# Tail of a fused cross-attention and state-space kernel: dummy products dropped, two comparisons reduced to a largest difference, five row tiles fetched ahead

## The chip, the core and the metric

The kernel runs on one core of a Trainium2 chip, in one launch. The metric is the device time of a whole execution in microseconds (us); where several executions were timed, the median stands for them. A profile of one further execution shows what each engine did: PE (the matrix engine; PEld is its weight load), DVE (vector), ACT (scalar), POOL (GpSimd) and SP, which issues nearly all DMAs.

## What is computed

```python
x = builder_state                       # 4096 x 512; base_state is 3202 x 512, 8 heads of 64
x1 = x + mha(layernorm(x), layernorm(base_state))        # softmax attention, then W_o
U = (layernorm(x1) @ W_in.T + b_in) @ Bmat               # 4096 x 64
def step(s, u_t):                       # one state of 64 numbers, 4096 steps in sequence
    s = silu(s @ A.T) + u_t
    return s, s
states = scan(step, zeros, U)
out = x1 + states @ Cmat + (program_probs.mean(1) @ W_prog.T + b_prog)
```

Everything is float32.

## The kernel before

**Attention.** The 4096 rows are cut into 8 blocks `Q` of 512 and each block into two halves; with 4 pairs of heads this gives 64 *units*, each of 13 *steps* over the keys. A step of a unit is a group of score products (`s`, line 1144), one exponential on ACT (`p`, line 1222), one addition on DVE (`acc`, line 1230) and a group of value products (`po`, line 1280). Keys and values come back from DRAM (`kd`, `vd`) step by step: `load_k` (line 432) is issued with the scores of ten steps earlier (`AHEAD_K`), `load_v` (line 440) six steps ahead of the scores (`AHEAD`), and the value product follows the scores by about four steps (`LAG`). In the last block the units run first over the first halves of the four head pairs and then over the second halves, and every unit loads its own keys and values.

**Rows.** The projected rows `x1`, with the modulation added, are stored in DRAM (`x1d`, lines 1732 and 1843). The inputs `U` of the scan stay in SBUF as `u`.

**The scan.** The 4096 steps are cut into 2 x 128 chunks of L = 16 steps, and all chunks advance together. A first sweep "a" (tile `za`) runs beside the last units from zero states and leaves a guess of each chunk's end in `end1`; a second sweep "b" (tile `z`) starts from those guesses, takes 16 steps `j`, and leaves its ends in `end0`. A step is a product on PE (line 1960), a tanh on ACT (line 1988) and a combination on DVE (line 1995). The last 256 rows, which the attention finishes last, have a short scan of their own (`zl`, `hl`, `sl`; pieces named `l.`).

**The output rows.** Row tile `j` (`rows[j]`, 128 x 2 x 512) holds the rows `16 c + j` of all chunks `c`, for `v` = 0 and 1, the two halves of the sequence; its `v` = 1 part has 112 rows, since the last 256 rows go another way. `fetch(j)` (line 1921) reads it from `x1d` after the last keys and values are loaded. When sweep "b" has finished step `j`, `states` (POOL, line 2027) and `products` (PE, line 2034) make the scan's share, and it is added to the row tile in one of two ways: for two of three `j`, ACT copies the `v` = 1 part (`copied`, line 2048) and POOL adds it (`added`, line 2051), and DVE adds the `v` = 0 part (`joined0`, line 2054); for the third, DVE adds both. SP stores both parts (line 2059). Products of even `j` lie in the PSUM tiles `py_n` and `py_o`, those of odd `j` in the two banks of one tile `pd_last`. The last 256 rows (`xr_l`) are made by two products (`last_ys`, line 2254), added on DVE (line 2257) and stored, the first half by SP and the second by ACT (line 2261).

**The check.** A program-wide number `nbad` says whether the guesses were good enough. `largest` (lines 2073 and 2074) takes the largest absolute value of the new ends and scales it by a tolerance into `top`; `differ` subtracts the old from the new (line 2079, DVE), takes absolute values (line 2081, ACT), compares each with `top` (line 2083, DVE) and counts (line 2084, DVE). This is done for "b" (128 columns) and for "l" (32 columns). `counted` (PE, line 2433) sums the counts over the partitions, `number` (line 2440) subtracts them from what they should be, and all engines load the result (line 2613) and branch past a general version when it is zero.

**What sets the order.** Each operation is a *piece* with an engine, an estimated cost, what it must follow, rings that it takes and a due time, shifted by a table. `Plan.order` simulates the engines with these numbers and writes the pieces out in the order in which the simulation starts them; each engine then executes its own pieces strictly in that order.

**Dummy products.** `idle_` (line 2239) multiplies `a_t` by itself into the scan's PSUM tile; three such pieces (`WARM` = 17 to 19) follow the last steps of the short scan and the end of sweep "b".

Of the kernel before, what the change touches and what calls it, by code (L numbers as in the profile page):

```python
# [13 lines left out]
AF = mybir.ActivationFunctionType  # L14
# [21 lines left out]
WARM = 17  # L36
# [6 lines left out]
NA = 7  # L43
HALF = 18
# [188 lines left out]
def xattn_ssm_kernel(  # L233
# [884 lines left out]
    def alt_tile(k, name):  # L1118
        return alt.tile([P, 2, H], F32, tag=f"alt{k}", name=name)
# [802 lines left out]

    def last_fetch():

        t = x_tile("xr_l")
        for g in range(2):
            r = LAST + g * P
            nc.sync.dma_start(t[:, g], x[r : r + P, :])
            xl.append(t[:, g])

    def open_scan():
# [15 lines left out]
        for name, n in (  # L1947
            ("end0", NCK + 1), ("end1", NCK + 1), ("ul", PRE + 1 + P), ("hw", P), ("hl", P),
            ("sl", P + 1), ("df", NCK), ("st", P // LT),
            ("top", 1), ("bad", 1), ("badl", 1), ("badr", 1),  # L1950
        ):
            sv[name] = two[:, at_ : at_ + n]
            at_ += n
# [122 lines left out]
    def differ(new, old, n, bad):  # L2076

        top, df, ok = sv["top"], sv["df"][:, :n], sv["ok"][:, :n]
        nc.vector.tensor_tensor(df, new, old, ALU.subtract)
        yield  # L2080
        nc.scalar.activation(df, df, AF.Abs)
        yield
        nc.vector.tensor_scalar(ok, df, top, None, ALU.is_le)
        nc.vector.tensor_reduce(bad, ok, AX.X, ALU.add)
# [32 lines left out]
    def last_rows(plan, d):  # L2117
# [121 lines left out]
        def idle_():  # L2239
            for k in range(2):  # L2240
                nc.tensor.matmul(sv["z"][1][:, k, :], a_t, a_t, start=True, stop=True)
# [98 lines left out]
    def drain(plan):  # L2340
# [66 lines left out]
        for name, new, old, count, bad, of in (  # L2407
            ("b", lambda: sv["end0"][:, 1:], lambda: sv["end1"][:, 1:], NCK, "bad", [("b", "end")]),
            ("l", lambda: sv["sl"][:, : P : LT], lambda: sv["st"], P // LT, "badl",
             [("l.near", 0), ("l.near", 1), "l.from", ("differ", "b", 2)]),  # L2410
        ):

            v = {}
# [23 lines left out]
        def number():  # L2437
            sv["nbad"] = small.tile([1, 1], I32, tag="nbad", name="nbad")
            all_ = P * (NCK + P // LT + 3 * len(units))
# [3 lines left out]
        plan.add("counted", "PE", 300, counted, ["risen", ("differ", "l", 2), *free[1]], d)  # L2443
# [169 lines left out]
    n = nc.values_load(sv["nbad"][0:1, 0:1], min_val=0, max_val=P * (NCK + P // LT + 3 * len(units)))  # L2613
# [88 lines left out]
```

## Time and profile before

| | us |
|---|---|
| median of 3 runs (lowest, highest) | 1889.19 (1888.89, 1890.3) |
| the profiled execution | 1889.67 |
| its span, first to last instruction | 1887.9 |
| outside the span | 1.77 |
| PE busy, DVE busy, ACT busy, POOL busy | 1873.1, 1563.3, 1166.6, 258.2 |

The profiled execution is 0.48 us above the median. PE's clock was granted at 0.999 over the span. Times in the text are from the start of the span. A row of the timeline gives start, duration, engine and line, operation, what is written and read, the count of instructions merged into it, and in brackets how long the engine had been idle and what ended that.

### The profile page before, as it was taken

The page shows a single profiled execution, that of the slowest core. Times are in us where ns is not written, and L with a number is a line of the kernel's source. Part 1 is how long each engine was busy: PE and PEld are TensorE (multiplying, and loading weights), DVE is VectorE, ACT ScalarE, POOL GpSimd, SP SyncE. Part 2 cuts the span into 40 slices and gives each one's busy share as a digit, 9 for nine tenths or more (in the row PEclk, how much of TensorE's full clock was granted, in tenths as well). Part 3 has the DMA queues.
Part 4 walks back from the last instruction along what each step waited for, and adds up shares of the span by engine and source line. Part 5 has one row for each costly group of instructions (what it writes and reads, how often), then busy time and mean ns, then how long its engine had stood idle before and what let it go on. Part 6 is the DMA issues. An engine that isn't in the chain of part 4 may idle for free.

```text
span 1887.9 us, 69209 instructions
## 1 busy us (share of the span) xinstructions
PE 1873.1 (99%) x29856; PEld 1414.9 (75%) x29856; DVE 1563.3 (83%) x2142; ACT 1166.6 (62%) x1663; POOL 258.2 (14%) x386
## 2 busy tenths in 40 slices
PE   9999999999999999999999999999999999999997
PEld 5887689777777777797777777777777777777684
DVE  6642699788988889798978898898979897989776
ACT  3242577665766577565756676757757575757653
POOL 6120300022000210022002200021002200110105
PEclk9999999999999999999999999999999999999999
DMA  8554133133323333233313332324313331536477
GB/s 257 158 159 120 54 102 92 38 115 90 106 74 105 86 112 97 65 95 111 98 44 108 87 114 79 106 79 117 98 55 98 107 104 44 171 108 182 139 190 238
DMA packets 260770, 207.58 MB, mean 110 GB/s; under 512 B 94632, under 2 KB 233896, under 8 KB 260460
## 3 DMA queue, kind: packets, MB, share of 16 engines
q1 hardware_dynamic: 256440, 196.48, 36.1%
q10 hardware_dynamic: 4020, 6.62, 1.2%
q8 instruction: 237, 3.88, 0.8%
q14 instruction: 73, 0.60, 0.1%
HBM read 156.32 MB, written 29.88 MB: 99 GB/s over the span
## 4 chain that ended last, share of the span: by engine, by line
PE 97%; DVE 1%; ACT 1%; DMA 0%; issue 0%; POOL 0%; SPq 0%; DVEq 0%; ACTq 0%; POOLq 0%
PE po L1280 37%; PE s L1144 36%; PE pax L404 3%; PE qx L404 3%; PE qy L404 2%; PE pay L404 2%; PE pkx L404 2%; PE pvx L404 2%; PE pvy L404 1%; PE pky L404 1%; PE pk L722 1%; PE pv L599 1%; PE pd L1309 1%; PE sm L1164 1%; PE po L1268 1%; PE pu L1747 1%
## 5 line engine op out<-in xcount | busy, mean ns | idle before, releaser
L1222 ACT ACTIVATE p<-s,shifts 128x1024 f32<-128x1024 f32 (+1 forms) x832 | 891.4, 1081 | 418.3 <-PE s L1144 392.7
L1230 DVE TENSOR_TENSOR acc<-p,acc 128x1024 f32<-128x1024 f32 (+1 forms) x704 | 851.0, 1214 | 96.8 <-ACT p L1222 77.2
L1144 PE MATMUL s<-q,k 64*64 64x256 f32 x12800 | 850.6, 376 | 0.2 <-ACT p L1222 0.2
L1280 PE MATMUL po<-p,v 64*64 64x256 f32 x12800 | 848.2, 376 | 1.0 <-DVE o L1335 0.9
L1144 PEld LDWEIGHTS s<-q,k 64*64 64x64 f32 x12800 | 518.9, 133 | 175.2 <-ACT p L1222 13.5
L1280 PEld LDWEIGHTS po<-p,v 64*64 64x64 f32 x12800 | 519.9, 133 | 163.1 <-issue 3.5
L1634 POOL TENSOR_TENSOR xr<-xr,rowb 128x512 f32<-128x512 f32 x28 | 35.7, 1274 | 797.6 <-DVE acc L1230 688.9
L1358 DVE RECIPROCAL rd<-rd 128x256 f32<-128x256 f32 (+1 forms) x64 | 110.0, 1719 | 6.4 <-ACT rd L1353 6.4
L1249 ACT COPY swap<-acc 64x256 f32<-64x256 f32 x126 | 50.8, 403 | 64.9 <-DVE acc L1237 61.8
L1230 DVE TENSOR_TENSOR acc<-p,p 128x1024 f32<-128x1024 f32 x64 | 78.2, 1222 | 11.6 <-ACT p L1222 11.5
L1729 POOL TENSOR_TENSOR xr<-x,modb 128x512 f32<-128x512 f32 x28 | 41.6, 1496 | 253.3 <-DVE acc L1254 178.3
L1420 POOL TENSOR_SCALAR rstd_x<-mv_x 128x1 f32<-128x1 f32 x28 | 18.6, 666 | 276.7 <-DVE mv_x L1417 276.0
L1215 DVE TENSOR_TENSOR acc<-x,acc 2x256 f32<-2x256 f32 x128 | 54.9, 429 | 1.5
L1254 DVE TENSOR_TENSOR acc<-swap,acc 64x256 f32<-64x256 f32 x126 | 52.4, 416 | 2.9 <-ACT swap L1249 1.3
L1570 ACT ACTIVATE q<-qx,bias 128x256 f32<-128x256 f32 x42 | 17.6, 470 | 48.0 <-PE qx L404 48.0
L582 DVE TENSOR_TENSOR ks<-pky,ks 128x512 f32<-128x512 f32 x15 | 10.4, 692 | 43.2 <-PE pky L404 23.7
L576 ACT ACTIVATE ks<-pkx,bias 128x256 f32<-128x256 f32 x40 | 16.8, 470 | 44.4 <-PE pkx L404 32.9
L1237 DVE TENSOR_TENSOR acc<-acc 128x512 f32<-128x512 f32 x63 | 43.1, 684 | 0.3
L1335 DVE TENSOR_TENSOR o<-po,o 128x256 f32<-128x256 f32 x64 | 27.0, 423 | 14.1 <-ACT o L1331 13.5
L481 DVE STREAM_TRANSPOSE x<-xh_y 128x512 f32<-128x512 f32 x28 | 18.2, 688 | 21.7 <-ACT xh_y L1428 14.7
L1353 ACT ACTIVATE rd<-pd 128x128 f32<-128x128 f32 x126 | 34.0, 275 | 1.0 <-PE pd L1309 0.4
L1178 DVE TENSOR_REDUCE m<-sm 128x1 f32<-128x256 f32 x64 | 24.0, 417 | 11.3 <-PE sm L1164 11.3
(314 smaller groups left out, 1760.7 us busy)
## 6 DMA issues: line engine op xcount, KB each, us to landing
k<-kd SPq DMA_DIRECT2D x432, 128.0 KB, 2.2
v<-vd SPq DMA_DIRECT2D x432, 128.0 KB, 2.2
xn<-x SPq DMA_DIRECT2D x448, 32.0 KB, 1.9
xr<-in_x_dram SPq DMA_DIRECT2D x30, 256.0 KB, 3.2
x1d<-xr SPq DMA_DIRECT2D x30, 256.0 KB, 2.2
x<-in_x_dram SPq DMA_DIRECT2D x28, 256.0 KB, 3.0
cx<-in_ctx_dram SPq DMA_DIRECT2D x25, 256.0 KB, 4.2
kd<-ks SPq DMA_DIRECT2D x20, 256.0 KB, 2.3
```

The lines of the kernel that those rows point to most:

```text
L404: nc.tensor.matmul(to[:, b, :], still[:, i, b * P : (b + 1) * P], moving[:, i, :], start=(start and b == 0 and i == 0), stop=(i == 1), ski ...
L1144: nc.tensor.matmul(s[k0 : k0 + HD, a, b, :], kts[(*w["at"][:2], c)][r, b * CK + k0 : b * CK + k0 + HD], q[r], start=True, stop=True, skip_ ...
L1215: made = nc.vector.tensor_tensor(to[r], t[r], to[r], ALU.add)
L1222: nc.scalar.activation(t[:, :, :nb, :], w["ps"][c][:, :, :nb, :], AF.Exp, bias=w["shift"])
L1230: return nc.vector.tensor_tensor(w["acc"][:, :, :nb, :], t[:, :, :nb, :], before[:, :, :nb, :], ALU.add)
L1237: return nc.vector.tensor_tensor(acc[:, :, 0, :], acc[:, :, 0, :], acc[:, :, 1, :], ALU.add)
L1249: nc.scalar.copy(w["swap"][r], of[(1 - k) * HD : (2 - k) * HD])
L1254: made = nc.vector.tensor_tensor(of[r], w["swap"][r], of[r], ALU.add)
L1280: nc.tensor.matmul(w["po"][k][a * HD : (a + 1) * HD, :QU], vts[Q, hp, c][r, b, a * HD : (a + 1) * HD], t[r, a, b, :], start=(c == 0 and b ...
L1358: nc.vector.reciprocal(w["rd"][:, part], (w["pd"] if last else w["rd"])[:, part])
L1634: return nc.gpsimd.tensor_tensor(xs[half][:, t], xs[half][:, t], rowb, ALU.add)
L1729: return nc.gpsimd.tensor_tensor(xt[:, t], x1[:, t], modb, ALU.add)
```

## The change

The diff has three parts.

1. **No dummy products.** `WARM`, `idle_` and its three pieces go.
2. **Comparisons by the largest difference.** `differ` becomes three DVE instructions in a row: the subtraction, a largest absolute value over the columns into one number a partition (`far`), and one comparison of `far` with `top`, whose result is the partition's count. ACT's absolute value, the comparison of all columns and the sum go, and what was three pieces for each comparison is one. The expected sum changes from `P * (NCK + P // LT + ...)` to `P * (2 + ...)`.
3. **Early rows.** For `j` = 0 to 4 (`NE`), `fetch_early` reads the `v` = 0 part and the first 96 rows of the `v` = 1 part while the last block is computed, as soon as the block before it has been stored and the tile's other users are done. `fetch_late` reads the other 16 rows at the old place.

```diff
-WARM = 17
+NE = 5
...
+    def fetch_early(j):
+
+        rows[j] = alt_tile(j, f"row_{j}")
+        for v, n in enumerate((NCK, END - QU // L)):
+            nc.sync.dma_start(rows[j][:n, v, :], x1r[v, j, :n])
+
+    def fetch_late(j):
+
+        c = slice(END - QU // L, END)
+        nc.sync.dma_start(rows[j][c, 1, :], x1r[1, j, c])
...
     def differ(new, old, n, bad):
 
-        top, df, ok = sv["top"], sv["df"][:, :n], sv["ok"][:, :n]
+        top, df, far = sv["top"], sv["df"][:, :n], sv["far"]
         nc.vector.tensor_tensor(df, new, old, ALU.subtract)
-        yield
-        nc.scalar.activation(df, df, AF.Abs)
-        yield
-        nc.vector.tensor_scalar(ok, df, top, None, ALU.is_le)
-        nc.vector.tensor_reduce(bad, ok, AX.X, ALU.add)
+        nc.vector.tensor_reduce(far, df, AX.X, ALU.max, apply_absolute_value=True)
+        nc.vector.tensor_tensor(bad, far, top, ALU.is_le)
...
-        def idle_():
-            for k in range(2):
-                nc.tensor.matmul(sv["z"][1][:, k, :], a_t, a_t, start=True, stop=True)
-
-        for t in range(WARM, PRE + LT):
-            plan.add(("l.idle", t), "PE", 430, idle_, [("l.z", t), ("b", "h", L - 1)], d)
...
+        before = NQB - 2
+        kept_rows_ = [("row", before, t, "store") for t in range(NT)]
+        used = [("sevenths", NQB - 1, k) for k in CHAIN], [("outs", before, k) for k in CHAIN]
+        for j in range(NE):
+            plan.add(("early", j), "SP", 1000, partial(fetch_early, j), kept_rows_ + used[int(j > 1)] + [from_(d - 36 * STEP)],
+                     d + (2 * j - 36) * STEP)
         for j in range(L):
-            plan.add(("fetch", j), "SP", 100, partial(fetch, j),
-                     ["fetch", ("product", n, j // 2)], d + (5 + j / 2) * STEP, ["p"] if j >= NA else [])
+            plan.add(("fetch", j), "SP", 100, partial(fetch_late if j < NE else fetch, j),
+                     ["fetch", ("product", n, j // 2)] + ([("early", j)] if j < NE else []),
+                     d + (5 + j / 2) * STEP, ["p"] if j >= NA else [])
...
-            def first(new=new, old=old, count=count, bad=bad, v=v):
+            def compare(new=new, old=old, count=count, bad=bad):
                 largest(new())
-                v["d"] = differ(new(), old(), count, sv[bad])
-                next(v["d"])
-
-            costs = (720, 280, 640) if count == NCK else (560, 200, 440)
-            for i in range(3):
-                plan.add(("differ", name, i), "ACT" if i == 1 else "DVE", costs[i],
-                         partial(lambda v, *_: next(v["d"], None), v) if i else first,
-                         [("differ", name, i - 1)] if i else of,
-                         d + (8 * STEP if name == "b" else 0))
+                differ(new(), old(), count, sv[bad])
+
+            plan.add(("differ", name, 0), "DVE", 1300 if count == NCK else 1050, compare, of, d + (8 * STEP if name == "b" else 0))
```

The order moves at three places only. On every engine, all instructions ahead of them stand as before.

The first place is DVE's last rows ahead of the loading of `nbad`. `row_24516` and `row_24519` are row tiles 14 and 15 before, `row_24521` and `row_24524` the same tiles now; `scan` holds all of the check's small tiles. Before:

```order
L2054 SCALAR_TENSOR_TENSOR row_24516<-py_o_24586,row_24516 112x512
L2073 TENSOR_REDUCE scan<-scan 128x1
L2079 TENSOR_TENSOR scan<-scan 128x128
L2054 SCALAR_TENSOR_TENSOR row_24516<-py_n,row_24516 128x512
L2083 TENSOR_SCALAR scan<-scan 128x128
L2054 SCALAR_TENSOR_TENSOR row_24519<-pd_last,row_24519 128x512
L2079 TENSOR_TENSOR scan<-scan 128x32
L2257 SCALAR_TENSOR_TENSOR xr_l<-py_a,xr_l 128x512
L2083 TENSOR_SCALAR scan<-scan 128x32
L2257 SCALAR_TENSOR_TENSOR xr_l<-py_o_24587,xr_l 128x512
L2440 TENSOR_SCALAR nbad<-pd_last 1x1
```

The same place on DVE now:

```order
L2065 SCALAR_TENSOR_TENSOR row_24521<-py_o_24591,row_24521 112x512
L2084 TENSOR_REDUCE scan<-scan 128x1
L2090 TENSOR_TENSOR scan<-scan 128x128
L2091 TENSOR_REDUCE scan<-scan 128x1
L2092 TENSOR_TENSOR scan<-scan 128x1
L2259 SCALAR_TENSOR_TENSOR xr_l<-py_a,xr_l 128x512
L2090 TENSOR_TENSOR scan<-scan 128x32
L2259 SCALAR_TENSOR_TENSOR xr_l<-py_o_24592,xr_l 128x512
L2065 SCALAR_TENSOR_TENSOR row_24521<-py_n,row_24521 128x512
L2065 SCALAR_TENSOR_TENSOR row_24524<-pd_last,row_24524 128x512
L2442 TENSOR_SCALAR nbad<-pd_last 1x1
```

Both additions into the `v` = 0 parts of tiles 14 and 15 moved behind both comparisons and both additions into `xr_l`; of each comparison only one of its several small rows is shown the second time. ACT's copy of tile 15 stood behind DVE's addition of tile 15 and waits for the products alone now, and that addition waits for the copy.

The second place is PE's end, from the last product of tile 14 on (`py_n`, `py_o`). Before:

```order
L2034 MATMUL py_o_24586<-c_21416,scan 64x256
L2241 MATMUL z<-a_t 128x128 x6
L2034 MATMUL pd_last<-c_21416,scan 64x256 x8
L2254 MATMUL py_a<-c_21416,scan 128x512
L2254 MATMUL py_o_24587<-c_21416,scan 128x512
L2433 MATMUL pd_last<-ones,scan 1x1 x3
```

PE's end now:

```order
L2045 MATMUL py_o_24591<-c_21416,scan 64x256
L2256 MATMUL py_a<-c_21416,scan 128x512
L2256 MATMUL py_o_24592<-c_21416,scan 128x512
L2045 MATMUL pd_last<-c_21416,scan 64x256 x8
L2435 MATMUL pd_last<-ones,scan 1x1 x3
```

The dummy products (`z<-a_t`) are gone, and the two products of the last rows moved ahead of the products of tile 15 (`pd_last`).

The third place is SP's queue in the last block, behind the store of a row tile of that block (`xr_23194`); `k_2_1_3` is the key load of head pair 2, second half, step 3. Now:

```order
L1843 DMA x1d<-xr_23194 128x512
L1927 DMA row_23495<-x1d 128x512
L1927 DMA row_23495<-x1d 96x512
L1927 DMA row_23530<-x1d 128x512
L1927 DMA row_23530<-x1d 96x512
L432 DMA k_2_1_3_23533<-kd 128x256
L440 DMA v_1_1_12_23535<-vd 128x128
L1927 DMA row_23559<-x1d 128x512
L1927 DMA row_23559<-x1d 96x512
L432 DMA k_2_1_4_23564<-kd 128x256
```

Before, the load of `k_2_1_3` followed the store directly; tiles 3 and 4 are fetched two and four pairs of loads later, ahead of `k_2_1_6` and `k_2_1_8`. At the old place, five DMAs of 16 rows stand where ten of 128 and 112 rows stood. At the very end of SP's queue, the `v` = 0 stores of tiles 14 and 15 moved behind the store of `xr_l` and the `v` = 1 store of tile 15, and are now the last two.

More of the change, by code (lines that the diff above doesn't have):

```diff
@@ L1949, in open_scan @@
             ("sl", P + 1), ("df", NCK), ("st", P // LT),
-            ("top", 1), ("bad", 1), ("badl", 1), ("badr", 1),
+            ("top", 1), ("far", 1), ("bad", 1), ("badl", 1), ("badr", 1),
         ):
@@ L2409, in drain @@
             ("l", lambda: sv["sl"][:, : P : LT], lambda: sv["st"], P // LT, "badl",
-             [("l.near", 0), ("l.near", 1), "l.from", ("differ", "b", 2)]),
+             [("l.near", 0), ("l.near", 1), "l.from", ("differ", "b", 0)]),
         ):
-            v = {}
-            def first(new=new, old=old, count=count, bad=bad, v=v):
+            def compare(new=new, old=old, count=count, bad=bad):
                 largest(new())
-                v["d"] = differ(new(), old(), count, sv[bad])
-                next(v["d"])
-            costs = (720, 280, 640) if count == NCK else (560, 200, 440)
-            for i in range(3):
-                plan.add(("differ", name, i), "ACT" if i == 1 else "DVE", costs[i],
-                         partial(lambda v, *_: next(v["d"], None), v) if i else first,
-                         [("differ", name, i - 1)] if i else of,
-                         d + (8 * STEP if name == "b" else 0))
+                differ(new(), old(), count, sv[bad])
+            plan.add(("differ", name, 0), "DVE", 1300 if count == NCK else 1050, compare, of, d + (8 * STEP if name == "b" else 0))
         def risen():
@@ L2438, in number @@
             sv["nbad"] = small.tile([1, 1], I32, tag="nbad", name="nbad")
-            all_ = P * (NCK + P // LT + 3 * len(units))
+            all_ = P * (2 + 3 * len(units))
             nc.vector.tensor_scalar(sv["nbad"], sv["py"][1][0][0:1, 0:1], -1.0, float(all_), ALU.mult, ALU.add)
         plan.add("risen", "DVE", 760, risen, [("fall", n), ("rise", n), ("l.kept", 1)], d + STEP)
-        plan.add("counted", "PE", 300, counted, ["risen", ("differ", "l", 2), *free[1]], d)
+        plan.add("counted", "PE", 300, counted, ["risen", ("differ", "l", 0), *free[1]], d)
         plan.add("number", "DVE", 150, number, ["counted"], d)
@@ L2612, in xattn_ssm_kernel @@
                     mybir.DependencyClass.Sync, mybir.DependencyReason.SCHED_ONLY), reason="shared port")
-    n = nc.values_load(sv["nbad"][0:1, 0:1], min_val=0, max_val=P * (NCK + P // LT + 3 * len(units)))
+    n = nc.values_load(sv["nbad"][0:1, 0:1], min_val=0, max_val=P * (2 + 3 * len(units)))
     with tc.If(n > 0, label="general"):
```

## The prediction

> **What bounds the kernel now.** I read the page first: engines, then the chain that ended last.
>
> ```profile
> span 1887.9 us, 69209 instructions
> PE 1873.1 (99%) x29856; PEld 1414.9 (75%) x29856; DVE 1563.3 (83%) x2142; ACT 1166.6 (62%) x1663; POOL 258.2 (14%) x386
> PE 97%; DVE 1%; ACT 1%; DMA 0%; issue 0%; POOL 0%; SPq 0%; DVEq 0%; ACTq 0%; POOLq 0%
> ```
>
> PE is busy for 99% of the span and makes 97% of the chain. No part of the change takes work from PE before 1875 us, and the order of every engine stands as before up to there but for SP. So there are two questions: do the early fetches on SP make PE wait, and what do the last ten microseconds lose or gain. Next I read the end of the timeline.
>
> ```profile
> 1875.96 1.60 PE L2241 MATMUL z<-a_t 128*128 128x128 f32 x12
> 1876.47 1.26 POOL L2051 TENSOR_TENSOR row<-y_l,row 112x512 f32<-112x512 f32 x1
> 1876.53 1.36 DVE L2001 TENSOR_TENSOR scan<-scan,u 128x128 f32<-128x128 f32 x1
> 1877.50 1.09 PE L2034 MATMUL pd_last<-c,scan 64*64 64x256 f32 x16
> 1878.52 0.69 PE L2254 MATMUL py_a<-c,scan 64*128 64x512 f32 x1
> 1878.70 0.28 DVE L2073 TENSOR_REDUCE scan<-scan 128x1 f32<-128x128 f32 x1
> 1879.02 0.15 DVE L2074 TENSOR_SCALAR scan<-scan 128x1 f32<-128x1 f32 x1
> 1879.09 0.28 DVE L2079 TENSOR_TENSOR scan<-scan 128x128 f32<-128x128 f32 x1
> 1880.40 0.68 DVE L2054 SCALAR_TENSOR_TENSOR row<-pd_last,row 128x512 f32<-128x512 f32 x1
> 1881.17 0.60 ACT L2048 ACTIVATE y_l<-pd_last 128x512 f32<-128x512 f32 x1 [1.46 <-DVE row L2054]
> 1881.85 1.26 POOL L2051 TENSOR_TENSOR row<-y_l,row 112x512 f32<-112x512 f32 x1 [4.12 <-ACT y_l L2048]
> 1882.02 1.13 DVE L2083 TENSOR_SCALAR scan<-scan 128x32 f32<-128x32 f32 x1
> 1883.18 0.19 DVE L2084 TENSOR_REDUCE scan<-scan 128x1 f32<-128x32 f32 x1
> 1883.29 0.68 DVE L2257 SCALAR_TENSOR_TENSOR xr_l<-py_o,xr_l 128x512 f32<-128x512 f32 x1
> 1883.88 0.14 DVE L2440 TENSOR_SCALAR nbad<-pd_last 1x1 int32<-1x1 f32 x1
> 1884.00 0.37 ACTq L2261 DMA_DIRECT2D out_dram<-xr_l  x1
> ```
>
> From 1878 us on DVE is the engine that ends last: it goes from one row to the next until 1883.97, and ACT then issues the last store. The rows of line 2261 and of SP's final waits say what follows.
>
> ```profile
> DMA to landing us min/median/max: 2.3/2.3/2.3
> L2614 SPq EVENT_SEMAPHORE  x8: 17/17/17, 1885.6 to 1886.5; - x8
> ```
>
> That store lands at 1884.00 + 2.3 = 1886.3; SP's eight waits for the DMA queues end right after it, at 1886.5, and the closing barrier ends the span at 1887.9. **The end is the landing of the last store plus 1.6 us**, and the last store hangs on DVE's last large addition.
>
> **Part by part.** *Early fetches.* They add ten DMAs to SP between the key and value loads. Each tile brings 128 + 96 rows of 2 KB, so the five bring 2.29 MB. Rows of the stages:
>
> ```profile
> 1765.00:1770.00 5.00, 5.00 (x116) 3.81 (x112) 3.17 (x4) 3.90 (x6) 0.00 (x0) 1.00 0.71 216
> 1770.00:1775.00 5.00, 5.00 (x88) 3.45 (x80) 4.58 (x5) 3.10 (x4) 0.00 (x0) 1.00 0.69 207
> 1775.00:1780.00 5.00, 5.00 (x95) 3.60 (x96) 4.57 (x4) 3.42 (x9) 1.28 (x1) 1.00 0.37 120
> 1825.00:1830.00 5.00, 5.00 (x103) 5.00 (x99) 5.00 (x7) 3.17 (x4) 0.00 (x0) 1.00 1.05 252
> 1766.53 0.38 SPq L432 DMA_DIRECT2D k<-kd  x1
> 1827.30 0.86 PE s L1144 x16
> 1828.16 0.86 PE po L1280 x16
> ```
>
> The last two columns are the share of the DMA engines and GB/s. Full DMA engines move 252 GB/s (1825 us), so 2.29 MB take 2.29 / 0.252 = 9.1 us of them. At 1765 to 1780 us they are not full, so I take 9.1 us as the most by which a load behind all ten fetches is late (the least is 0, if the free share takes them all); ten issues of 0.38 us lie within it. What hides it is the lead of the loads. A step costs PE 0.86 + 0.86 = 1.72 us; keys are issued ten steps ahead, 17 us, and values six steps and the lag of four, also 17 us. 17 − 9.1 leaves 8 us, so I take **0** from a range of 0 to 9.1, and PE stays at 5.00 of 5.00. At the old place, 1816 to 1844 us, SP's row of fetches becomes shorter:
>
> ```profile
> 1816.41 27.85 SPq L1921 DMA_DIRECT2D row<-x1d  x32
> POOL xr_l L2349 <- DMA xr_l<-in_x_dram: 41.7, 1, 41.7
> 1851.94 0.68 DVE L2054 SCALAR_TENSOR_TENSOR row<-py_n,row 128x512 f32<-128x512 f32 x1
> ```
>
> The first tile is added at 1851.94, more than seven microseconds after the last fetch was issued (1816.41 + 27.85 = 1844.3), and the only wait for a DMA among all waits from 1815 us to the end is that of `xr_l`, which is fetched ahead of the rows in both versions. Nobody waits for the rows, so earlier rows gain **0**.
>
> *Dummy products.* Twelve matmuls of 1.60 us go at 1875.96. They stood ahead of tile 15's products, whose inputs were there by about 1876.6: the last of them, DVE's addition of tile 13, stands just ahead of L2001, and the states just ahead of POOL's row at 1876.47. The two products of the last rows take the dummies' place. How long until PE starts what follows them no row shows; the last of them begins to end 0.69 us after the start, and tile 15's 16 matmuls held PE for 1.02 (1877.50 to 1878.52), so it is between these and I take 1.0. They run from 1875.96, tile 15's products then from 1877.0 to 1878.1, **0.5 us earlier** than 1877.50 + 1.09. Does the clock hold without them? It is the number ahead of the last two in each row:
>
> ```profile
> 1881.00:1882.00 1.00, 0.17 (x2) 0.09 (x2) 0.97 (x5) 0.71 (x2) 0.15 (x1) 1.00 0.87 322
> 1883.00:1884.00 1.00, 0.24 (x4) 0.14 (x4) 0.96 (x4) 0.00 (x0) 0.11 (x1) 0.86 0.79 297
> ```
>
> PE's last large products began at 1878.52; the clock is still full at 1881 to 1882 and falls between 1883 and 1884. After the change no gap of a microsecond lies ahead of tile 15's products, so I take 0. [...]
>
> *The copy of tile 15.* ACT's copy no longer stands behind DVE's addition (it started at 1881.17 for that reason). It starts right behind tile 15's products, at about 1878.15, and ends 0.60 later, and POOL's addition starts 0.08 after it (1881.85 against 1881.77 before): 1878.85 to 1880.1. Before, it lay at 1881.85 to 1883.11.
>
> *The shared stall.* While POOL adds two SBUF tiles, some DVE instructions stand still. L2001 took 1.36 us, and L2083 took 1.13, and both ended right after POOL did. An earlier place tells which kinds do:
>
> ```profile
> 1703.54 2.51 POOL L1729 TENSOR_TENSOR xr<-x,modb 128x512 f32<-128x512 f32 x2
> 1704.96 0.38 DVE L1361 TENSOR_REDUCE rises<-rd 128x1 f32<-128x256 f32 x1
> 1705.26 1.07 DVE L1369 TENSOR_TENSOR o<-o,rd 128x256 f32<-128x256 f32 x1
> 1827.77 0.41 DVE L1369 TENSOR_TENSOR o<-o,rd 128x256 f32<-128x256 f32 x1
> ```
>
> A reduction beside POOL takes no longer; a TENSOR_TENSOR from SBUF waits until POOL is done (1.07 against 0.41 us). L2083's stall goes: 1.13 less some 0.2, as 32 columns take (the reduction at 1883.18 took 0.19), is 0.93. But the subtraction of comparison "b" would start at 1879.09 and meets POOL's addition at its new place: it ends about 1880.25 instead of 1879.37. **The stall of 0.93 us goes and one of 0.9 us comes**: 0 together.
>
> *DVE's remaining work.* From 1878.70 on the same additions are left in both versions, so I count the difference. The comparisons of all columns go, 0.28 (as for the subtraction of 128 columns) and 0.2. The sums become largest differences over the same columns, 0. Two comparisons of one column come; no row shows one, the nearest is the 128x1 TENSOR_SCALAR of 0.15, with 0 and the 0.28 of 128 columns as bounds: + 0.3. An instruction that needs the one ahead starts 0.04 after its end (1878.70 + 0.28, then 1879.02), one that doesn't starts 0.08 before it (1879.17, then 1879.09); two more pairs are of the first kind now, 2 × 0.12 = + 0.24. Together − 0.48 + 0.30 + 0.24 = + 0.06, and with the stalls + 0.03: **DVE ends where it ended**, at 1884.0.
>
> *The last store.* It was the second half of `xr_l`, issued alone; the store ahead of it was issued 0.86 us earlier. Now three stores of 256 KB are ready within 1.3 us (`xr_l` at about 1882.7, tile 14 at 1883.4, tile 15 at 1884.0). Rows:
>
> ```profile
> 1883.14 0.33 SPq L2059 DMA_DIRECT2D out_dram<-row  x1
> 1882.00:1883.00 1.00, 0.01 (x1) 0.00 (x0) 1.00 (x2) 0.00 (x0) 1.00 (x1) 1.00 0.83 320
> DMA to landing us min/median/max: 3.1/3.7/5.0
> ```
>
> At 320 GB/s a store of 262 KB costs 0.82 us, three cost 2.5. Behind each other they push the last landing from 2.3 us after its issue to between 2.3 (no queue) and 3.1 (the least of the stores of line 2059 after 1870 us). I take 2.7, between the two, since the queue is short by then: +0.4. Tile 15's store also sits on a queue that SP waits for early, so more of the eight waits follow it: about +0.1.
>
> *The count.* `counted` writes where tile 15's addition reads, so it follows it now: if its six tiny matmuls take half a microsecond, `nbad` ends near 1884.7 instead of 1884.02. From there to SP's first wait at 1885.6 was 1.6 us, so the waits begin near 1886.3, ahead of the landing at 1886.7: covered, 0.
>
> **Sum** against the profiled execution: fetches 0, DVE's end 0, landing 0.4 and waits 0.1, together +0.5, 1889.67 to 1890.2. That execution lay 0.48 above the median of 1889.19, so for the median I say **1889.7 us**.
>
> **Rivals.** (a) *The stall misses.* If ACT's copy comes later and POOL starts behind the subtraction, only the one-column comparison can meet it; DVE ends up to 0.9 us earlier and the stores spread out: −0.5 us, 1888.7. For it: 0.25 us decide. Against it: even then POOL holds until 1880.6 and the comparison of "b" waits.
>
> (b) *The early fetches starve PE* (slower). SP is one queue, and loads stand behind fetches. Once a load is held up so long that it lands after its lead of 17 us, PE loses a microsecond for each further one. For it: the DMA engines are at 0.7 already, and a landing takes some 2.3 us beside the hold-up (as at line 2261). Against it: the bytes are worth 9.1 us. It decides from a hold-up of 17 − 2.3 = 14.7 us on; at two and a half times 9.1, it gives 22.8 + 2.3 − 17 = +8: 1897.
>
> (c) *The dummies were needed.* If PE's clock falls to half without them, the products of the last rows and of tile 15 take twice 1.0 and 1.09: +2.1, 1891.8. For it: PE has pauses all through the tail. Against it: the rows on the granted clock above.
>
> (d) *Faster*: less DMA traffic from 1816 to 1844 lets some access in the tail run quicker. No wait in the profile shows one; the row tiles would have to be late by 4 us, and 1889.2 − 4 = 1885.2 results.
>
> **How the numbers follow.** Forecast 0.60, (a) 0.25, (b) 0.06, (c) 0.05, (d) 0.04. Within 0.2% means within 3.8 us, about what a measurement of this kernel can tell from no change; the forecast, (a) and (c) lie there. Faster 0.04, same 0.89, slower 0.07. The range takes in (a) with the runs' own spread of 0.3 below, the forecast with a full queue at the end (+0.4 more, and 1.1 of spread above): 1888.4 to 1891.2.
>
> **What would show it.** POOL's last addition near 1879 to 1880 and the subtraction beside it at 1.1 us instead of 0.28 (the stall); the last matmuls of tile 15 done near 1878.1; DVE's last large addition ending at 1884.0, with a landing 2.7 us later; PE at 5.00 of 5.00 from 1765 to 1815 us. It is wrong if PE waits for a key or value after 1766 us, if the subtraction takes 0.28 us, or if the clock falls below 1.00 before 1878 us.

## The result, and the profile after

The changed kernel takes **1891.98 us** (median of 21 runs, 1891.17 to 1892.86), the kernel before took 1889.14 us beside it (21 runs, 1888.77 to 1890.76). The ratio is 1.0014, with a 95% interval from 1.0008 to 1.0020: 2.84 us slower, and outside the range of the prediction. The profiled execution took 1892.13 us; these are two lines of its page.

```profile
span 1890.3 us, 69189 instructions
PE 1870.7 (99%) x29844; PEld 1413.6 (75%) x29844; DVE 1562.8 (83%) x2142; ACT 1167.0 (62%) x1661; POOL 258.2 (14%) x386
```

The span grew by 2.4 us while PE does less than before. So the loss isn't work; it must be looked for in the order and the waits of the end. The timeline of the changed kernel's last 15 us (start, duration, engine, line, operation, tiles):

```profile
1875.61 1.35 DVE L2012 TENSOR_TENSOR scan<-scan,u 128x128 f32<-128x128 f32 x1
1876.11 1.09 PE L2045 MATMUL pd_last<-c,scan 64*64 64x256 f32 x16
1877.33 0.60 ACT L2059 ACTIVATE y_l<-pd_last 128x512 f32<-128x512 f32 x1
1878.00 1.26 POOL L2062 TENSOR_TENSOR row<-y_l,row 112x512 f32<-112x512 f32 x1 [1.19 <-ACT y_l L2059]
1878.17 1.24 DVE L2090 TENSOR_TENSOR scan<-scan 128x128 f32<-128x128 f32 x1
1879.77 0.16 DVE L2092 TENSOR_TENSOR scan<-scan 128x1 f32<-128x1 f32 x1
1882.01 0.37 ACTq L2263 DMA_DIRECT2D out_dram<-xr_l  x1
1882.49 0.68 DVE L2065 SCALAR_TENSOR_TENSOR row<-pd_last,row 128x512 f32<-128x512 f32 x1
1883.55 0.15 DVE L2442 TENSOR_SCALAR nbad<-pd_last 1x1 int32<-1x1 f32 x1 [0.38 <-PE pd_last L2435]
```

The order is the one that was set out with the change, and the subtraction beside POOL's addition took 1.24 us. But `nbad` ends at 1883.70, which is 0.32 us earlier than before, and still the span ends 2.4 us later. What lies between are only the load of `nbad` by every engine, the branch on it, and the closing barrier. These are SP's own waits from 1884.5 us on, first of the kernel before, then of the changed one (waiting line, what ended the wait, us in total, times, longest):

```profile
SPq L2614 <- SPq L2614: 0.9, 2, 0.5
SPq L2698 <- PEq L2698: 0.6, 2, 0.5
```

```profile
SPq L2700 <- PEq L2616: 2.6, 1, 2.6
SPq L2700 <- PEq L2700: 0.6, 2, 0.5
SPq L2616 <- SPq L2616: 0.5, 1, 0.5
```

A wait of 2.6 us for PE's sequencer is new: in the barrier, SP waits for PE, which has nothing left to compute. Line 2616 (2614 before) is the `tc.If`. Its rows give each engine's branch (durations in ns), the changed kernel's first, then PE's of before:

```profile
L2616 ACTq COMPARE_BRANCH  x1: 76/76/76, 1884.9 to 1884.9; - x1
L2616 POOLq COMPARE_BRANCH  x1: 65/65/65, 1884.9 to 1884.9; - x1
L2616 PEldq COMPARE_BRANCH  x1: 4310/4310/4310, 1885.0 to 1885.0; - x1
L2616 DVEq COMPARE_BRANCH  x1: 90/90/90, 1885.0 to 1885.0; - x1
L2616 SPq COMPARE_BRANCH  x1: 70/70/70, 1885.3 to 1885.3; - x1
```

```profile
L2614 PEldq COMPARE_BRANCH  x1: 415/415/415, 1884.9 to 1884.9; - x1
```

**PE's branch took 4.31 us where it had taken 0.42.** Put together, from the trace's records:

| point | before | after | difference |
| --- | --- | --- | --- |
| the last step's addition (L2001, L2012) starts | 1876.53 | 1875.61 | −0.92 |
| `nbad` ends | 1884.02 | 1883.70 | −0.32 |
| PE's branch starts | 1884.92 | 1885.00 | +0.08 |
| PE's branch ends | 1885.34 | 1889.31 | +3.97 |
| the last store lands | 1886.29 | 1885.64 | −0.65 |
| the span ends | 1887.89 | 1890.35 | +2.46 |

Before, the end hung on the last landing (1.6 us ahead of it); now it hangs on PE's branch (1.0 us ahead of it), and the stores have long landed. What is PE's sequencer doing for 4.3 us? One view offers an answer, the DMA queues. On the page of the changed kernel:

```profile
q8 instruction: 237, 3.88, 0.9%
q14 instruction: 73, 0.60, 0.1%
```

q8 moved 3.88 MB in 237 packets of 16 KB; PE executes 2 × 29844 products and weight loads, so that is 65 bytes for each. So q8 very likely brings PE's code, by this estimate some 250 instructions a packet. Now the same view of the window from 1874 to 1884 us (packets, MB, share), first before, then after:

```profile
q14 instruction: 2, 0.02, 0.7%
q8 instruction: 1, 0.02, 0.6%
```

```profile
q14 instruction: 2, 0.02, 0.4%
```

Before, a packet of PE's code came at 1879.43, five microseconds ahead of the branch. In the changed kernel none came between 1871.23 and the branch; the next one starts at 1886.03, 1.03 us after the branch began, and ends at 1887.94.

### The profile page after: what moved, and what is told of

Read it like the earlier page. It is cut to its first block, busy times and chain, and to the rows that moved or that the text cites. A ratio compares the mean times of both kernels' runs of the same rounds, so it can differ in the third digit from the quotient of the medians.

```text
span 1890.3 us, 69189 instructions
## 1 busy us (share of the span) xinstructions
PE 1870.7 (99%) x29844; PEld 1413.6 (75%) x29844; DVE 1562.8 (83%) x2142; ACT 1167.0 (62%) x1661; POOL 258.2 (14%) x386
## 3 DMA queue, kind: packets, MB, share of 16 engines
q8 instruction: 237, 3.88, 0.9%
## 4 chain that ended last, share of the span: by engine, by line
PE 97%; DVE 1%; ACT 1%; issue 0%; DMA 0%; POOL 0%; SPq 0%; DVEq 0%; ACTq 0%; POOLq 0%
PE po L1280 36%; PE s L1144 36%; PE pax L404 3%; PE qx L404 3%; PE qy L404 2%; PE pay L404 2%; PE pkx L404 2%; PE pvx L404 2%; PE pvy L404 1%; PE pky L404 1%; PE pk L722 1%; PE pv L599 1%; PE pd L1309 1%; PE sm L1164 1%; PE po L1268 1%; PE pu L1747 1%
```

## Theories, and what the experiments had to tell apart

- **F (code).** PE jumps at the branch to code that isn't there. The change takes six products, 24 instructions, out of PE's stream, so a fetch that used to come before the branch now comes after it.
- **C (clock).** Without dummies PE is idle from 1877 us on; its clock is granted at half (0.51 in the mean of 1880 to 1885 us, 0.87 before), and it wakes up slowly.
- **S (stores).** The comparisons move three stores to the end, and their landing or their order costs the time.

In all diffs below, line numbers and names are those of the kernel that each starts from. "PE's branch" is the duration of its COMPARE_BRANCH in the run's profile, and a landing is the moment at which a store reports its end; the medians stand beside that of before in the same series.

### One part at a time

Without the dummies alone (a2):

```diff
-WARM = 17
+WARM = 20
```

> The kernel before without its six dummy products in the tail, nothing else. Theory F: 24 instructions fewer ahead of the branch, TensorE's branch takes 4.3 us and the time is 2 to 2.9 us above before, 1891.2 to 1892.0. Rival C expects the same here. Rival S (what the new comparisons and the new order of the stores do): within 0.5 us of before, since both stay as they were.

Measured: 1891.39 us against 1889.16 (ratio 1.0011, 1.0002 to 1.0020), branch 4.24 us. Taking out the dummies is enough.

The changed kernel with the dummies put back (a3; the diff restores `idle_` and its plan entries from before):

> The changed kernel with the six dummy products of before put back in the tail (comparisons and early rows as changed). Theory F and rival C: branch 0.4 us, time 1888.6 to 1889.6. Rival S: above 1891.

Measured: 1891.90 against 1889.16 (1.0014, 1.0005 to 1.0023), and yet the branch took 0.41 us. Theory F's time was missed by over 2 us, though its branch was right: something else costs as much there. Theory C, which expected the same, missed by as much. The rows of its last stores (line 2071 from 1883.2 us on; ns of the issue, then us to landing):

```profile
L2071 SPq DMA_DIRECT2D out_dram<-row x2: 398/410/423, 1883.1 to 1883.6; - x2
DMA to landing us min/median/max: 2.3/3.8/5.2
```

The last store, issued at 1883.58, landed 5.2 us later, at 1888.74. So theory S has a case too.

The new comparisons alone (a7: `largest` and `differ` of the change with before's dummies and fetches) and the early rows alone (a8):

> The kernel before with the new comparisons alone (dummies and row fetches as before): TensorE's stream has the same length, so its branch takes 0.4 us by either theory F. Rival S (the new order of VectorE's last work, all stores late and close together, delays the landing of the last store, as in the run with the dummies put back, where the last store was issued at 1883.58 and landed at 1888.74): time 1890.5 to 1892 with the last landing over 4 us after its issue. If that landing was not due to the comparisons: within 0.5 us of before, 1888.7 to 1889.7.

> The kernel before with the early rows alone (dummies and comparisons as before). TensorE's branch takes 0.4 us. If the pause of 0.43 us that TensorE made in before at 1834.5 us (absent in the changed kernel) comes from the rows' fetches beside it, it is gone: time 1888.5 to 1889.0. If it was chance: 1889.0 to 1889.4. If the early rows are what cost: above 1890.

Measured: a7 1891.69 against 1889.13 (1.0012, 1.0003 to 1.0021; its runs lie from 1891.34 to 1892.72), branch 0.41 us, last store issued 1883.77, landed 1889.34. a8 1889.16 against 1889.13 (1.0000, 0.9991 to 1.0009), branch 0.50 us. So **two parts cost 2.2 and 2.6 us alone, by two different stalls, and 2.84 together**; the third costs nothing. The two don't add up, because the second stall is absent from the changed kernel: without the dummies, the last rows' products stand ahead of tile 15's, the additions into `xr_l` come earlier (1879.84 and 1881.29 in the changed kernel, 1882.14 and 1882.74 in a7), and the last store lands at 1885.64.

### Where PE's instructions stand (theories F and C)

The kernel before with fewer dummies at the program's start (a4), then the changed kernel with tiny products more at the start (a1 six, a6 five, b1 ten):

```diff
-        for _ in range(11):
+        for _ in range(5):
             nc.tensor.matmul(idle[:, :P], a_t, a_t, start=True, stop=True)
```

```diff
+        for _ in range(6):
+            nc.tensor.matmul(idle[0:1, :1], a_t[:, 0:1], a_t[:, 0:1], start=True, stop=True)
```

> The kernel before with 5 instead of 11 dummy products at the start of the program (24 TensorE instructions fewer there), the tail with all its dummies. Theory F: where the instructions are taken out doesn't matter, so TensorE's branch takes about 4.3 us and the time is 2 to 3.5 us above before (what the start itself gains or loses by the missing dummies is read from its profile, at most 3 us). Rivals C and S: the branch stays at 0.4 us, and only the start can change the time.

> The changed kernel with six tiny products (1x1 results, 24 TensorE instructions) more among the dummies at the start of the program; the tail is as changed, without dummies. Theory F (code fetch: the change takes 24 instructions out of TensorE's stream ahead of the branch, so the 16 KB block of code that holds the branch's target isn't fetched yet when the branch comes): TensorE's COMPARE_BRANCH takes 0.4 us instead of 4.3, a fetch on queue q8 stands again some us ahead of it, the span falls by about 2.5 us and the time to 1889.0 to 1889.8. Rival C (TensorE is idle from 1877 to 1883 without the dummies and wakes slowly, its clock is granted at half): the branch stays at 4.3 us, the time at 1892.0. Rival S (the last stores or their order): 1892.0 as well.

> The changed kernel with five tiny products (20 TensorE instructions) more at the start: TensorE's stream ahead of the branch is 3 instructions shorter than in before, where a1_pad24 made it 1 longer. [...] Theory F2 (place in the tail) and rival C: branch 4.3 us, time 1891.5 to 1892.3.

> The changed kernel with ten tiny products (40 TensorE instructions) more at the start, 17 instructions more ahead of the branch than before has. So far all 10 executions with 24 more in the tail took 1889.4 to 1890.0, 5 of 11 with 24 more at the start took 1889.9 to 1890.1 and the other six 1892, 1 of 10 with 20 more took 1889.7, and none of 21 with none more. Theory F1' (the number of instructions ahead of the branch decides, with an edge that is blurred by a few instructions, near 24): all executions near 1889.9, branch 0.4 to 0.5 us. Theory F2 (only instructions that pass in the tail count): most near 1892, as with 24 at the start.

And the changed kernel with six (a5) or three (b2) tiny products in the tail, ahead of tile 15's:

```diff
+        def ys_():
+            last_ys("a")
+            for _ in range(6):
+                nc.tensor.matmul(sv["z"][1][0:1, 0, 0:1], a_t[:, 0:1], a_t[:, 0:1], start=True, stop=True)
```

> The changed kernel with six tiny products (1x1 results, 24 TensorE instructions, under 0.3 us in all) in the tail, between the sequence's last products and those of tile 15; VectorE's order is that of the changed kernel. So far: TensorE's branch took 0.41 us in before and with the dummies put back, and 4.2 to 4.7 us in the changed kernel, in before without the dummies, in before with 24 instructions fewer at the start, and also in the changed kernel with 24 more at the start. Theory F1 (only the number of instructions ahead of the branch counts, and lies here where it lay with 24 more at the start): branch 4.3 us, time 1892. Theory F2 (the fetch of the block with the target starts only if instructions pass TensorE's sequencer in the tail, near the end): branch 0.4 us, span 2.5 us shorter than the changed kernel's, time 1889.0 to 1889.8. Rival C (dummies are needed to keep TensorE busy): 0.3 us of tiny products leave TensorE idle for 6 us as before, branch 4.3 us, 1892.

> The changed kernel with three tiny products (12 TensorE instructions) in the tail, half of a5_tail24. Theory F1' (edge near 24, wherever they stand): branch over 4 us, all or nearly all executions at 1891.5 to 1892.3. Theory F2, if a few instructions in the tail are enough: 1889.4 to 1890.0 as with 24.

| run | PE instructions against the changed kernel | PE's branch, us | median, us | quick executions |
| --- | --- | --- | --- | --- |
| changed kernel | 0 | 4.31 | 1891.98 | 0 of 21 |
| a6 | +20 at the start | 4.45 | 1892.10 | 1 of 10 |
| a1 | +24 at the start | 4.27 | 1891.95 | 5 of 11 |
| b1 | +40 at the start | 0.50 | 1890.12 | 10 of 10 |
| b2 | +12 in the tail | 0.50 | 1889.45 | 9 of 10 |
| a5 | +24 in the tail | 0.50 | 1889.71 | 10 of 10 |

("Quick" are the executions up to 1890.4 us; the others begin at 1891.17, with nothing between.) The branch was read in the profiled execution alone; that the quick executions had a quick branch is inferred from their times. a4 took 1894.34 against 1889.16 (1.0028, 1.0018 to 1.0039), 5.2 us more where F said 2 to 3.5: its first value product (`po`) starts 1.8 us later (205.35 against 203.58; with fewer dummies ahead of them, the first eight products of line 599 took 5.74 us instead of 4.30), and its branch took 4.72 us **although all dummies of the tail are there**. That goes against C, and so does the clock itself, in these rows of the window from 1880 to 1885 us (the number ahead of the last two is the granted clock). First a1, whose branch took 4.27 us, then a3, where it took 0.41:

```profile
1880.00:1885.00 5.00, 0.29 (x6) 0.19 (x6) 3.45 (x11) 0.00 (x0) 0.00 (x0) 0.77 0.88 310
```

```profile
1880.00:1885.00 5.00, 0.29 (x6) 0.18 (x6) 3.18 (x10) 0.00 (x0) 0.00 (x0) 0.63 0.58 212
```

The slower clock goes with the quicker branch. And a5's 24 tiny instructions stand ahead of tile 15's products, so PE is idle behind these nearly as long as in the changed kernel (5.4 us against 6.0 ahead of the count). In all profiles of this study but the three d runs below, seventeen, a quick branch goes with a packet on q8 that starts between 1877.6 and 1879.5 us (eleven profiles), and a slow one with none there (six). The strict form of F, in which only the number of instructions ahead of the branch counts, fell with a1 and a6, though: a1 has one instruction more than before and was slow in six of eleven executions, b2 has eleven fewer and was quick in nine of ten.

### The target of the branch (theory F), and the late landing (theories S and L)

After a7, theory S was made sharper: **L**, the last store's completion is held up by the code that the engines fetch once they have branched. a7's queues, from 1886.8 to 1887.22 us:

```profile
q14 instruction: 4, 0.03, 21.3%
q8 instruction: 1, 0.02, 14.9%
q1 hardware_dynamic: 13, 0.01, 9.6%
```

All five fetches of code stand among the last 13 packets of the store; from 1887.22 to 1889.34, when it lands, no packet starts at all. If the fetches are to blame, a later branch must help. b3 is a7, and b4 the kernel before, with 2 us of useless work ahead of `nbad`:

```diff
             sv["nbad"] = small.tile([1, 1], I32, tag="nbad", name="nbad")
+            for _ in range(7):
+                nc.vector.tensor_tensor(sv["df"], sv["end0"][:, 1:], sv["end1"][:, 1:], ALU.subtract)
```

> The kernel before with the new comparisons, and seven subtractions of 128x128 of VectorE (0.28 us each, 2.0 us, into scratch) ahead of the last count, so that every engine's branch comes 2.0 us later while the stores stay where they are. Theory L (in the new order the last store's final packets, near 1887.2, meet the fetches of code that the engines' branches ask for, and its landing comes 2.1 us after its last packet instead of 0.35): with the branches later the fetches begin after 1887.5, the last store lands by 1887.6 instead of 1889.34, and the kernel with 2 us more work is faster than a7_compare, 1890.4 to 1891.4 against 1891.7. Rival (the late landing belongs to the stores themselves, three of them close together): landing stays near 1889.3, and the time is 1891.7 or, where the branches come last, up to 1892.

> The kernel before with the same seven subtractions ahead of the last count. In before the last store lands 1886.3, 0.35 us after its last packet, already ahead of most fetches, so nothing is gained by a later branch: 1.2 to 2.0 us slower than before, 1890.3 to 1891.1, by theory L and by its rival.

Measured: b3 1890.97 against 1889.24 (1.0009, 1.0000 to 1.0019), so with 2 us of work more it is 0.7 us faster than a7 (nine of its ten executions lie below all eleven of a7); b4 1890.74 (1.0009, 0.9999 to 1.0019), 1.5 us slower than before. The stores of a7 and b3 were issued at the same places (the last at 1883.77 and 1883.82). Line 2059 in a7, then in b3 (the last store's us to landing), and b3's queues from 1887.21 to 1889.3 us:

```profile
DMA to landing us min/median/max: 5.6/5.6/5.6
```

```profile
DMA to landing us min/median/max: 3.4/3.4/3.4
```

```profile
q14 instruction: 4, 0.03, 5.4%
q8 instruction: 1, 0.02, 3.4%
```

In b3 the same five fetches come behind the landing, and the store is 2.2 us faster. But 3.4 us without a fetch beside it is still more than the 2.3 of the last store before: that much is left for S, which no run here tests alone.

What remained open was the cause in PE's case. The next runs cut the block that the branch jumps over, which these inputs never enter, so no executed instruction ahead of the branch changes: c1 (changed kernel), c2 (a7) and c3 (before) leave `attend()` out of it, d1, d2 and d3 the whole block but for one copy.

```diff
     with tc.If(n > 0, label="general"):
-        attend()
```

The d runs instead (all other lines of the block go too):

```diff
     with tc.If(n > 0, label="general"):
-        attend()
...
+        nc.vector.tensor_copy(sv["sl"][:NS, 0:1], sv["end0"][NS:, END : END + 1])
```

> The changed kernel without the attention part of the general block (the block behind the last branch that is entered only when the check fails, which these inputs never do): TensorE jumps over some 650 instructions instead of some 3000; no executed instruction differs. Theory F (TensorE waits for the code at the branch's target, which lies beyond what has been fetched): the target is now within the code fetched in sequence, branch 0.5 us or less, time 1889.2 to 1889.8. Rival (the 4.3 us belong to the branch itself or to TensorE's idle and slow clock): branch 4.3 us, 1892.

> The kernel before with the new comparisons, and the same part of the general block left out. Theory L (the last store's completion waits behind the fetches that follow the branches): if the shorter jumps need no fetch, the last store lands 0.35 us after its last packet, near 1887.5, and the time is 1889.6 to 1890.2 instead of 1891.7. If fetches still follow the branches, they meet the store as before, 1891.7. Rival (three stores close together land late by themselves): landing near 1889.3, 1891.7, whether fetches follow or not.

> Control: the kernel before with the same part of the general block left out. Its branch is quick already and its end is the landing of the last store (1886.3) plus 1.6 us: 1888.6 to 1889.4 by every theory; a gain of more than 0.5 us would show that the branches cost it something too.

Measured: c1 1891.72 against 1889.08 (1.0013, 1.0004 to 1.0023), branch 4.24 us; c2 1891.50 (1.0012, 1.0003 to 1.0022), with the fetches still there (five from 1886.82 on) and the landing at 1888.57; c3 1889.11 (1.0004, 0.9994 to 1.0013). The branch over some 650 instructions was as slow (4.24 us) as the one over some 3000 (4.31).

c3 limits theory L: four of its fetches began between 1885.46 and 1885.66 us, its last store's last packet started at 1885.72, and the store landed only 0.33 us behind it. So a fetch among the last packets doesn't always hold a store up. (c3's last store is ACT's, of four late packets on another queue; that of a7 and c2 is SP's.)

> The changed kernel with the whole general block left out but for one copy of VectorE (these inputs never enter it): TensorE's branch jumps over a handful of instructions. No executed instruction ahead of the branch differs. Theory F (TensorE waits for code that hasn't been fetched): branch 0.5 us or less, time 1889.2 to 1889.8. Rival (the 4.2 us belong to the branch, or to TensorE idle and at half clock): branch 4.2 us, time 1891.5 to 1892.3.

> The kernel before with the new comparisons, and the general block left out in the same way. Theory L (the last store's completion waits behind the fetches of code after the branches): fewer or no fetches among the last store's packets, landing 0.35 us after the last packet, near 1887.5, time 1889.6 to 1890.2 instead of 1891.7. Rival (three stores close together land late by themselves): 1891.7.

> Control: the kernel before with the general block left out in the same way. Its end hangs on the landing of the last store (1886.3) plus 1.6 us, and its branch was quick: 1888.6 to 1889.4 by every theory.

Measured: d1 1889.46 against 1889.40 (0.9997, 0.9988 to 1.0007), d2 1890.10 (1.0006, 0.9996 to 1.0015), d3 1888.85 (0.9998, 0.9989 to 1.0008). PE's branch in d1, and then, from d2, the last store's landing and SP's longest wait at the end:

```profile
L2616 PEldq COMPARE_BRANCH  x1: 258/258/258, 1885.0 to 1885.0; - x1
```

```profile
DMA to landing us min/median/max: 3.4/3.4/3.4
```

```profile
SPq L2656 <- DMA out_dram<-row: 0.6, 1, 0.6
```

With one copy of DVE left in the block, PE's branch took 0.26 us and q8 brought no packet from 1874 us to the end of the span, PE as idle as in the changed kernel (0.29 us of matmuls from 1880 to 1885 us in both): **F is shown, C is not the cause**. In d2 no code is fetched within the span after 1874 us, and the last store lands 3.4 us after its issue, as in b3: **L is shown** for a7 by two interventions that left the order and the spacing of its stores as they were. S doesn't fall with it: d2 is 1.25 us slower than d3, without any fetch in either, and its last store lands at 1886.72 us where d3's lands at 1885.62. Nor is every long execution explained: four of d2's ten took 1891.0 to 1892.2 us, two of c3's ten 1892.0 and 1892.3, and three of the 25 of before beside the d runs 1891.7 to 1892.2; only one execution of each kernel was profiled, so it stays open what held these. (Of the times of d1 to d3, more than usual lies behind the span: d1's is 1887.0 us long in an execution of 1889.41, 2.4 us more; before it is 1.8. So the span shows the gain better than the time.)

None of these versions beats the kernel before. Of those with a part of the change and the whole general block, the quickest are a8 and b2, at 1889.16 and 1889.45 us, which can't be told from before (1.0001, 0.9991 to 1.0010 for b2).

## Why the prediction was wrong, step by step

- **Early fetches, 0: right.** a8 measured 0, and in the changed kernel PE stays busy for 5.00 of 5.00 us where the rows arrive, with the DMA share at 1.05:

```profile
1770.00:1775.00 5.00, 5.00 (x88) 3.44 (x84) 4.58 (x5) 3.57 (x4) 0.02 (x1) 1.00 1.05 263
```

- **Dummy products, tile 15 earlier by 0.5 us: right.** Its products start 1.39 us earlier (1877.50, 1876.11), of which 0.92 is the lead that the execution already had (0.44 of it a pause of PE in the execution of before, told of at the end). The clock held up to there, as forecast: 1.00 from 1875 to 1880 us, the products again 1.09 us. So rival (c) is wrong in its mechanism, though its 1891.8 is nearly the time measured.
- **Copy, stall, comparisons: right.** With the lead of 0.92 added back, POOL's last addition lay at 1878.92 to 1880.18 (forecast 1878.85 to 1880.1), the subtraction took 1.24 us instead of 0.28 (forecast 1.1), and DVE's last large addition ended at 1884.09 (forecast 1884.0).
- **The last store, 2.7 us: nearly.** Line 2070's last store landed 2.4 us after its issue, since `xr_l`'s second half had gone 1.2 us earlier.

```profile
DMA to landing us min/median/max: 2.4/2.4/2.4
```

- **The count, "covered, 0": this step failed.** `nbad` ended at 1884.62 with the lead added back, as forecast (1884.7). But the prediction let everything behind it run as before, 1.6 us to SP's first wait and the barrier after that. Two parts of that were wrong. The load of `nbad` took twice as long (line 2615, then 2613 of before, ns):

```profile
L2615 PEldq TENSOR_LOAD <-nbad x1: 990/990/990, 1883.9 to 1883.9; - x1
```

```profile
L2613 PEldq TENSOR_LOAD <-nbad x1: 490/490/490, 1884.2 to 1884.2; - x1
```

So SP came to its eight waits half a microsecond later than worked out, and found the last store already landed (1885.64). This is the changed kernel's row:

```profile
L2616 SPq EVENT_SEMAPHORE  x8: 17/17/17, 1885.8 to 1886.4; - x8
```

The count was not covered, then, even before the branch comes in: where the branch is quick (a5, b1, b2), the end follows `nbad` by 4.07 to 4.11 us, 3.87 in before. The larger part is PE's branch, which the sum put at nothing without giving a reason: 3.9 us more on PE, of which SP's barrier step waits 2.6. None of the rivals had it, because PE was taken to be finished with its last product; the eight waits of SP and the barrier were read only for the stores. In the kernels where the branch took 0.26 to 0.50 us and the rest is the changed kernel's (a5, b1, b2, d1) the medians are 1889.45 to 1890.12, around the forecast of 1889.7. That the number fits there is partly luck: the prediction reached it by the landing of the last store, and in a5, b1 and b2 the way from the count decides.

What the traces show of the cause is this. q8's packets are of 16,384 bytes each. In before one came from 1879.43 to 1880.35 us, 4.6 us ahead of the branch's start, and the branch took 0.42 us; in the changed kernel one came 1.03 us into the branch, which took 4.31; in d1 none came from 1874 us on, and it took 0.26. c1's expectation took the target for fetched once it lay some 650 instructions on. That was the author's estimate, and the branch of 4.24 us goes against it; how far ahead of the branch PE's code had been fetched, no run shows.

**What stays open:** which event lets PE's code be fetched ahead of the branch. In these runs more instructions ahead made it likelier (at the start 1 of 10 executions was quick with 20 more, 5 of 11 with 24, 10 of 10 with 40), and fewer did it in the tail (12: 9 of 10), but the rule isn't found. Each engine executed one BRANCH_PREFETCH_HINT, at 0.7 to 0.8 us; it did so alike in all twenty profiles, so by itself it doesn't tell quick from slow. Open too is how a fetch holds a store up: in a7 the last fetch ended at 1888.19 us and the store landed 1.15 us after that, and c3's store was not held.

## What to carry to other kernels

Here six products that compute nothing were worth 2.2 us (a2) through PE's branch, which took 4.24 us without them and 0.42 with them; when such a line is taken out or put in, look at every engine's branch and at the instruction queues ahead of it, not only at what the line computed or kept warm. Read the end of a program to its last barrier and ask of each engine, the idle ones too, what it must still do to get there. And where the last transfer decides, look at what the branches set off beside it: here the earlier branch made the end later (a7 took 1891.69 us, b3, whose branches come 2 us later, 1890.97).

## What the runs showed of the hardware that was not expected

- TensorE's branch took 4.2 to 4.7 us in the six profiles without a packet on q8 from 1874 to 1884 us, 0.41 to 0.51 us in the eleven with a packet there that starts between 1877.6 and 1879.5 us, and 0.25 to 0.26 us in d1 to d3, with one copy of DVE between it and its target. The other engines' branches took 0.07 to 0.09 us in every run.
- Three stores whose last packets ran among the engines' fetches of code landed 1.45 to 2.14 us after their last packet (c2: 1887.12 and 1888.57, a3: 1886.99 and 1888.74, a7: 1887.20 and 1889.34); c3's did too and landed 0.33 us after it. Elsewhere it was 0.33 to 0.36 us (before: 1885.93 and 1886.29, b3: 1886.88 and 1887.21).
- An engine's load of one number, `nbad`, took 0.48 to 0.54 us in b4, 0.49 to 0.76 in before, 0.89 to 0.99 in the changed kernel and up to 1.2 in a7; what sets it wasn't tested.
- With the rows fetched at the old place, PE lost 0.3 to 0.5 us ahead of its last value products in four of ten profiles (the first to the last such product: 1631.80 to 1631.96 us instead of 1631.5 to 1631.6); with the early rows in none of ten. Four of ten against none may be chance, and in the times of a8 it can't be seen.
